# Attention and spectral mixing on one core: the rotary table of the first rows placed ahead of the shift, the first load in four pieces, projections ordered by halves, and three fills placed behind a normalization

## The chip, the core and the metric

The kernel runs on one core of a Trainium2 chip. Five engines work side by side, each through its own queue in order: TensorE (PE) multiplies matrices into PSUM, VectorE (DVE) and ScalarE (ACT) do elementwise work and reductions, GpSimd (POOL) does elementwise work and issues part of the DMAs, and SyncE (SP) only issues DMAs. The metric is the device time of one execution in microseconds (us), as the median of several runs.

## The reference

The input x has shape (2, 2048, 256). Each row is normalized to mean 0 and variance 1. The normalized rows xn go through causal attention with 16 query heads and 4 key and value heads of 16 numbers, with rotary position encoding, and through a spectral mixing layer. Both results are added to x. Cut to what matters:

```python
xn = _layernorm(x)                                   # rows of 256
q, k, v = xn @ wq, xn @ wk, xn @ wv                  # 16, 4 and 4 heads of 16
q, k = _apply_rope(q, cos, sin), _apply_rope(k, cos, sin)
scores = einsum('bshd,bthd->bhst', q, k) / sqrt(16)  # causal, softmax over t
attn_out = einsum('bhst,bthd->bshd', softmax(scores), v) @ wo
y = real(ifft(einsum('bnd,do->bno', fft(xn), w_re + 1j * w_im))) + bias
out = x + attn_out + y
```

## The kernel before

**Blocks and units.** The rows are cut into 8 blocks of 512 (`blocks`, line 78), ordered by position first, so that blocks 0 and 1 are the first 512 rows of the two sequences, blocks 2 and 3 the next 512, and so on. A block is a tile `xt` of 128 partitions with 4 groups (`NI`) of 256 columns. The 16 heads of a block are worked off in 4 units of 4 heads (`units`, line 591). For each unit, TensorE first makes scores with queries on the partitions, from which VectorE takes the row maxima (`maxima`, line 593; tile `sm`). The maxima then enter the second score product as additional rows (`spread`, line 668), whose exponentials ScalarE takes (`scores`, line 693), and `values` (line 767) multiplies them with v.

**From a block of x to queries and keys.** `load_x` (line 166) brings a block in with one DMA from SyncE's queue. `row_stats` (line 233) takes mean and variance on VectorE, one group of 128 rows at a time. `row_power` (line 241) takes the reciprocal root on GpSimd. `row_shift` (line 247) makes the shift on VectorE. `project` (line 379) then holds the pieces of a block: `norm` (four instructions, on VectorE for block 0, on GpSimd for the others), `transpose_x` (TensorE, for each half of the 256 columns, copied by ScalarE into `xnT`), `features` (three products, for K with V and for two halves of Q; each sums over both halves of `xnT`), `other_half` (rotary partners of a feature; with a permutation product in blocks 0 and 1, with DMAs in later ones), `proj_v` (transposes v into the tile `va`), `rotate` and `split` (the rotation and the parting of a float32 into three bfloat16 numbers, seven instructions for each of the three features, on VectorE for block 0, on GpSimd for the others). The parts go by DMA from SyncE's queue into stacked tiles `kst` and `qst` (`stack`, `stack_runs`). `ones` (line 370) fills `va` and four pieces of `kst` of a block with the number one beforehand, on VectorE for block 0 and on GpSimd for the others.

**Tables.** `rotary_table` (line 276) makes the cosines and sines of 512 positions: `expand` on VectorE, eight reductions that read the loaded angles `trig`, and `turn` on TensorE, transposes that ScalarE copies into `cs`. `spectral_matrix` (line 315) makes one matrix out of the two Fourier transforms and the weights, in six pieces on TensorE. `load_late` (line 217) issues the loads for it and for the output product from GpSimd's queue.

**What sets the order.** The order of instructions on each engine is written by a planner when the program is built. It keeps a planned time for each engine (`clock`), planned times at which data or buffers are there (`there`), and rings of buffers (`slots`): the n-th tile of a ring with m buffers waits for the (n-m)-th. `use` adds an instruction's planned cost, `send` that of a DMA, `through_bank` that of a product with the copy of its PSUM bank; the ring `st` of PSUM banks has three. Up to line 1006 instructions are put down as the code reads: a warm-up of 48 transposes on TensorE (line 997), `ones(0)`, statistics, root, late loads, shift, weights. Then `chain` (line 1008) and `table` (line 1033) put the pieces of blocks and tables into streams. A piece has a step of attention from which it may go (`since`), one by which it is due (`by`), its engine, the data that it needs, and the rings from which it takes a buffer. The loop from line 1127 picks the next piece. Off TensorE it takes the piece that could start soonest, and among those within 0.1 us on the same engine the one that is due first. On TensorE it prefers, in turns that depend on how far ScalarE and VectorE are, scores ("B"), row maxima ("A"), due pieces ("F"), values ("V") and pieces that are not due yet ("M"). The chip's engines then follow this order, whatever the real times are.

The pieces of block 0 are due before step 0, those of block 1 by step 1 or a few steps later; the pieces of a later block on TensorE may go in steps `s["pe"] + k // 2`, where k counts them in their list.

Of the kernel before, what the change touches and what calls it, by code (L numbers as in the profile page):

```python
# [23 lines left out]
def tile_attn_plus_spectral_ffn(  # L24
# [29 lines left out]
    nc = tc.nc  # L54
# [11 lines left out]
    NI = SB // P  # L66
# [37 lines left out]
    def slot(tag, more=0):  # L104

        return tag, used[tag] + more - ring[tag]
# [57 lines left out]
    xt = {}  # L164

    def load_x(n):
        send("sp", 512, [slot("xt")], [("xt", "in", n)])
        take_slot("xt")
        xt[n] = work.tile([P, NI, D], F32, tag="xt", bufs=2, name=f"xt{n}")
        nc.sync.dma_start(out=xt[n], in_=block_rows(n))  # L170

    take_slot("qst"), take_slot("qst")
    load_x(0)
# [55 lines left out]


    rstd, shift, mv = {}, {}, {}

    def row_stats(n, i):
        if i == 0:
            mv[n] = work.tile([P, NI, 2], F32, tag="mv", bufs=2, name=f"mv{n}")
        st = work.tile([P, 6], F32, tag="bn", bufs=3, name=f"bn{n}_{i}")
        nc.vector.bn_stats(st, xt[n][:, i, :])
        nc.vector.bn_aggr(mv[n][:, i, :], st)
        use("dve", 0.53, [("xt", "in", n)], [("mv", n)])

    def row_power(n):
        rstd[n] = work.tile([P, NI], F32, tag="rs", bufs=2, name=f"rs{n}")
        nc.gpsimd.tensor_scalar(rstd[n], mv[n][:, :, 1], EPS, None, ALU.add)
        nc.gpsimd.tensor_tensor(rstd[n], rstd[n], neg_half, ALU.pow)
        use("pool", 1.35, [("mv", n)], [("rs", n)])

    def row_shift(n):
        shift[n] = work.tile([P, NI], F32, tag="sh", bufs=2, name=f"sh{n}")
# [27 lines left out]
    def rotary_table(j):  # L276
        ex = []

        def expand():
            at = []  # L280
            for a in range(2):
                ex.append(work.tile([P, NI, P], F32, tag="raw", bufs=3, name=f"trx{j}_{a}"))
                at.append(slot("raw"))
                take_slot("raw")
            for f in range(2):
                for a, e, k in ((0, 0, 0), (0, 1, 0), (1, 0, 2), (1, 1, 1)):
                    cols = f * HP + e * QD
# [5 lines left out]
                    nc.vector.tensor_reduce(  # L293
                        ex[a][:, :, cols : cols + QD].rearrange("p i (d h) -> p i d h", h=NKV),
                        wide.unsqueeze(4), AX.X, ALU.max,
                    )
            use("dve", 1.15, at, [("trx", j)])
            there["trx slots", j] = used["raw"]

        def turn(a):  # L300
            if a == 0:
                cs[j] = work.tile([P, 2, SB], F32, tag="cs", bufs=2, name=f"cs{j}")
            ps = bank(f"ps_tr{j}_{a}")
            for i in range(NI):
                nc.tensor.transpose(ps[:, i * P : (i + 1) * P], ex[a][:, i, :], ident)
# [62 lines left out]
    xnT, va, kst, qst = {}, {}, {}, {}  # L368

    def ones(n):  # L370
        e, eng, us = (nc.vector, "dve", 2.7) if n == 0 else (nc.gpsimd, "pool", 2.5)
        va[n] = const.tile([P, NI, NKV, QD], F32, tag=f"va{n}", name=f"va{n}")
        e.memset(va[n], 1.0)
        kst[n] = const.tile([P, NKV, SB], BF16, tag=f"kst{n}", name=f"kst{n}")
        for h in range(NKV):
            e.memset(kst[n][96:P, h, :], 1.0)
        use(eng, us, (), [("ones", n)])

    def project(n):
# [1 line left out]

        b, j = blocks[n]
        e, eng = (nc.vector, "dve") if n == 0 else (nc.gpsimd, "pool")
        MULT, SUB, CAST, NORM = (0.72, 0.72, 0.46, 0.33) if n == 0 else (1.23, 1.13, 0.63, 0.53)
        raw, sw, swp, part, ra, at = {}, {}, {}, {}, {}, {}
        sends = []
        streams.append(sends)

# [27 lines left out]
            if c == NK - 1:  # L416
                there["xt", n] = clock["pe"]

        def features(c):
            ps = bank(f"ps_q{n}_{c}")  # L420
            for k in range(NK):
                product(
                    ps, wp[:, k, c, :], xnT[n][:, k, :], start=(k == 0), stop=(k == NK - 1)
                )
            raw[c] = work.tile([P, SB], F32, tag="raw", bufs=3, name=f"raw{n}_{c}")
            at[c] = take_slot("raw")
            nc.scalar.copy(raw[c], ps)  # L427
            through_bank(
                1.83, ["wp", *(("xnT", n, k) for k in range(NK))], "act", 0.48, [("raw", "in", n, c)],
                [("raw", at[c] - ring["raw"])],  # L430
            )
            if n >= 2:
                other_half(c)
# [568 lines left out]
        row_stats(0, i)  # L1002
    row_power(0)
    load_late()
    row_shift(0)
    order_weights()

    def chain(n, starts, late=0):

        norms, pe, rot = project(n)  # L1010
        eng = norms[0][0]
        stats = [("dve", [("xt", "in", n)], [], lambda i=i: row_stats(n, i)) for i in range(NI)]
# [273 lines left out]
```

## Time and profile before

| What | us |
|---|---|
| median of 3 runs | 926.1 (925.84 to 926.69) |
| profiled execution, its own time | 926.6 |
| span of that profile, from first to last instruction | 924.9 |
| TensorE busy | 904.8 |
| VectorE busy | 749.3 |
| ScalarE busy | 654.3 |
| GpSimd busy | 370.2 |
| first row maxima product that waits for stacked queries starts at | 32.58 |

The profile describes one execution. In a timeline, each row has the start and the duration in us, the engine (PE is TensorE's products, PEld its weight loads), the line of the kernel, the operation, the tile written and the tiles read, the shape, and how many like instructions the row holds. Brackets give the idle time of the engine before the row and what ended it. In rows of windows, the engines' busy times are followed by the granted clock of TensorE (1.00 is full speed), the busy share of the DMA engines and the rate in GB/s. Matmuls overlap, so that a busy TensorE isn't always at its peak.

### The profile page before, as it was taken

What the parts mean: (1) busy time and instruction counts of PE and PEld (TensorE: products, weight loads), DVE (VectorE), ACT (ScalarE), POOL (GpSimd) and SP (SyncE); (2) the same over time, 40 slices, a digit from 0 to 9 for tenths busy, and PEclk for the clock granted to TensorE, in tenths of its full rate; (3) what the DMA queues carried; (4) which work ended last, traced back from release to release, by engine and by line L of the source; (5) the groups of instructions that cost most, each with busy time, mean ns of one, the idle gap of its engine ahead of it and who ended that gap; (6) DMA issues with size and microseconds to landing.
All of it is one profiled execution on the core that took longest, in us unless ns stands there. A gap on an engine that the chain in (4) does not pass through costs nothing.

```text
span 924.9 us, 39006 instructions
## 1 busy us (share of the span) xinstructions
PE 904.8 (98%) x17324; PEld 499.3 (54%) x17324; DVE 749.3 (81%) x1062; ACT 654.3 (71%) x1381; POOL 370.2 (40%) x556
## 2 busy tenths in 40 slices
PE   7999899999999999999999999999999999999997
PEld 4655565655555555555555555555455554645443
DVE  6878697789779997898995999979789989788601
ACT  3266665588757784888865777858687878588785
POOL 7287666824672414822246520311571021102121
PEclk9999999999999999999999999999999999999999
DMA  5435724351244011440002510010133001100000
GB/s 162 122 88 139 201 84 115 89 141 39 60 117 133 27 38 31 115 128 26 15 27 85 140 38 14 27 60 14 28 107 93 15 3 38 48 15 14 28 1 24
DMA packets 42024, 62.13 MB, mean 67 GB/s; under 512 B 8872, under 2 KB 32152, under 8 KB 41856
## 3 DMA queue, kind: packets, MB, share of 16 engines
q1 hardware_dynamic: 32432, 41.18, 16.7%
q0 software_dynamic: 8128, 17.69, 5.9%
q8 instruction: 135, 2.21, 1.0%
q10 hardware_dynamic: 1296, 0.79, 0.3%
q14 instruction: 33, 0.27, 0.1%
HBM read 32.75 MB, written 18.40 MB: 55 GB/s over the span
## 4 chain that ended last, share of the span: by engine, by line
PE 89%; DVE 4%; ACT 3%; issue 1%; DMA 1%; SPq 1%; POOL 1%; ACTq 0%; DVEq 0%; POOLq 0%
PE av L782 24%; PE st L155 22%; PE sm L155 17%; PE sm L631 7%; PE po L155 6%; PE ps_q L155 4%; DVE mx L636 2%; PE sp L155 2%; PE sm L627 2%; PE st L738 1%; ACT es L745 1%; PE ps_x L411 1%; PE st L734 1%; ACT es L747 1%; SPq L393 1%
## 5 line engine op out<-in xcount | busy, mean ns | idle before, releaser
L636 DVE TENSOR_REDUCE mx<-sm 128x2 f32<-128x1024 f32 (+3 forms) x640 | 649.1, 1058 | 87.7 <-PE sm L631 45.0
L745 ACT ACTIVATE es<-st 128x512 f32<-128x512 f32 (+3 forms) x1194 | 552.4, 543 | 179.7 <-PE st L155 145.5
L155 PE MATMUL st<-qst,kst 115*32 115x512 bf16 (+3 forms) x4264 | 327.1, 354 | 1.1 <-ACT es L745 0.4
L782 PE MATMUL av<-es,va 128*32 128x512 f32 (+3 forms) x2560 | 299.3, 530 | 0.8 <-issue 0.5
L155 PE MATMUL sm<-kst,qst 112*32 112x512 bf16 x3072 | 239.1, 379 | 0.1
L155 PEld LDWEIGHTS <-kst 115*32 115x32 bf16 x4608 | 160.8, 95 | 140.0 <-issue 64.1
L752 POOL TENSOR_SCALAR_AFFINE_SELECT es<-es 128x256 f32<-128x256 f32 x192 | 76.7, 407 | 274.9 <-ACT es L745 233.4
L155 PEld LDWEIGHTS <-qst 112*32 112x32 bf16 x3072 | 96.0, 96 | 93.0 <-issue 65.0
L631 PE MATMUL sm<-kst,qst 112*32 112x32 bf16 (+15 forms) x2048 | 122.0, 280 | 0.8 <-DMA qst<-part 0.8
L627 PE MATMUL sm<-mask,ident_h 128*32 128x64 bf16 (+3 forms) x2048 | 100.0, 201 | 1.2 <-DVE mx L636 0.9
L782 PEld LDWEIGHTS av<-es,va 128*32 128x32 f32 x2560 | 84.7, 109 | 28.3 <-ACT avs L796 2.6
L631 PEld LDWEIGHTS <-qst 112*32 112x32 bf16 x2048 | 66.1, 97 | 34.3 <-issue 20.7
L627 PEld LDWEIGHTS <-ident_h 128*32 128x32 bf16 x2048 | 66.0, 96 | 32.9 <-issue 26.0
L931 DVE TENSOR_TENSOR xr<-po,xr 128x256 f32<-128x256 f32 x36 | 15.3, 424 | 52.3 <-PE po L155 50.4
L817 POOL DMA_DIRECT2D res<-avs x30 | 18.2, 606 | 81.9 <-ACT avs L796 79.3
L155 PE MATMUL ps_q<-xnT,wp 128*32 128x512 f32 x384 | 45.5, 602 | 0.0
L747 ACT ACTIVATE es<-sp 128x1024 f32<-128x1024 f32 (+3 forms) x43 | 36.5, 907 | 7.3 <-PE sp L155 7.2
L427 ACT COPY raw<-ps_q 128x512 f32<-128x512 f32 x24 | 14.1, 586 | 35.1 <-PE ps_q L155 33.9
L518 POOL TENSOR_TENSOR ra<-raw,cs 128x512 f32<-128x512 f32 (+1 forms) x21 | 27.5, 1307 | 24.2 <-ACT raw L427 23.0
L738 PE MATMUL st<-qst,kst 115*32 115x160 bf16 (+15 forms) x512 | 36.4, 281 | 0.4 <-issue 0.4
L155 PE MATMUL po<-wo_sb,attT 128*32 128x256 f32 x512 | 35.0, 380 | 0.7 <-ACT attT L892 0.7
L734 PE MATMUL st<-mask_t,ident_h 128*32 128x128 bf16 (+3 forms) x512 | 30.6, 202 | 4.2 <-issue 3.3
(113 smaller groups left out, 663.0 us busy)
## 6 DMA issues: line engine op xcount, KB each, us to landing
qst<-run SPq DMA_DIRECT2D x62, 128.0 KB
res<-avs POOLq DMA_DIRECT2D x30, 256.0 KB, 2.9
run<-part SPq DMA_DIRECT2D x31, 192.0 KB
qst<-run SPq DMA_DIRECT2D x31, 192.0 KB
xt<-in_L_attn_x_dram SPq DMA_DIRECT2D x8, 512.0 KB
xr<-in_L_attn_x_dram SPq DMA_DIRECT2D x16, 256.0 KB
sw<-raw SPq DMA_DIRECT2D x60, 64.0 KB
attT<-res POOLq DMA_DIRECT2D x15, 256.0 KB, 4.2
```

The lines of the kernel that those rows point to most:

```text
L155: nc.tensor.matmul(to[q : q + QD], lhsT[:, q : q + QD], rhs, start=start, stop=stop)
L518: e.tensor_tensor(ra[c][:r], raw[c][:r], cs[j][:r, 0, :], ALU.mult)
L627: nc.tensor.matmul(to[:, at:wd], ident_h[:, q : q + QD], mask[:, q:], start=True, stop=True, skip_group_check=True,)
L631: nc.tensor.matmul(to[:, : at + QD], rows[:, q : q + QD], keys[:, : at + QD], start=False, stop=True, skip_group_check=True,)
L636: nc.vector.tensor_reduce(t["mx"][:, i, 2 * pr : 2 * pr + 2, k], ps[0][:, :, :wd], AX.X, ALU.max)
L734: nc.tensor.matmul(to[:, lo : at + QD], ident_h[:, q : q + QD], mask_t[:, : q + QD], start=True, stop=True, skip_group_check=True,)
L738: nc.tensor.matmul(to[:, at:], keys[:, q : q + QD], rows[:, at:], start=False, stop=True, skip_group_check=True,)
L745: nc.scalar.activation(es[u, t, pr][:, e, lo:], ps[:, lo:], AF.Exp, scale=SCALE)
L747: nc.scalar.activation(es[u, t, pr][:, :, lo:], wide[pr][:, :, lo:], AF.Exp, scale=SCALE)
L752: nc.gpsimd.affine_select(out=es[u, t, pr][:, :, lo : lo + P], in_=es[u, t, pr][:, :, lo : lo + P], pattern=[[0, 2], [1, P]], compare_op=A ...
L782: nc.tensor.matmul(av[u][QD * h : QD * (h + 1), lo:], va[at_block[b, t // NI]][:, t % NI, h, :], es[u, t, h // 2][:, h % 2, lo:], start=(t ...
L817: nc.gpsimd.dma_start(out=res[n, c][f], in_=avs[u])
```

## The change

The change has these parts.

- `load_x` loads block 0 with four DMAs of 128 rows each, instead of one of 512 rows. Each group's statistics depend on its own DMA. The other blocks keep one DMA.
- The table of the first 512 positions is expanded (`expand`) between `load_late` and `row_shift(0)` in VectorE's order. Before, the planner put it behind `row_shift(0)`.
- `features` becomes a piece for each half of the 256 columns. The first half takes the PSUM bank and needs only the first half of `xnT`, the second half needs the second one and ends with ScalarE's copy. The list of pieces of a block grows by three.
- `ones` of blocks 1, 2 and 3 (and of later ones) needs the last normalized group of block 1, so that the planner puts these fills behind block 1's normalization in GpSimd's order.
- Planned costs change: statistics from 0.53 to 0.6, root from 1.35 to 1.6, `expand` from 1.15 to 1.6, fills on GpSimd from 2.5 to 2.9, normalization of block 1 from 0.53 to 0.8, and two more sends are planned in `load_late`. A half of a feature is planned at 0.9, a whole one was at 1.83.

```diff
     def load_x(n):
-        send("sp", 512, [slot("xt")], [("xt", "in", n)])
+        at = slot("xt")
         take_slot("xt")
         xt[n] = work.tile([P, NI, D], F32, tag="xt", bufs=2, name=f"xt{n}")
-        nc.sync.dma_start(out=xt[n], in_=block_rows(n))
+        step = NI if n else 1
+        for i in range(0, NI, step):
+            send("sp", 128 * step, [at], [("xt", "in", n, k) for k in range(i, i + step)])
+            nc.sync.dma_start(out=xt[n][:, i : i + step, :], in_=block_rows(n)[:, i : i + step, :])
...
         nc.gpsimd.dma_start(out=bias_sb, in_=bias.partition_broadcast(P))
+        send("pool", 256, (), ())
+        send("pool", 128, (), ())
...
-        def features(c):
-            ps = bank(f"ps_q{n}_{c}")
-            for k in range(NK):
-                product(
-                    ps, wp[:, k, c, :], xnT[n][:, k, :], start=(k == 0), stop=(k == NK - 1)
-                )
+        def features(c, k):
+            if k == 0:
+                held[c] = bank(f"ps_q{n}_{c}"), take_slot("st")
+            ps, at_st = held[c]
+            product(ps, wp[:, k, c, :], xnT[n][:, k, :], start=(k == 0), stop=(k == NK - 1))
+            use("pe", 0.9, ["wp", ("xnT", n, k), ("st", at_st - ring["st"])], [("ps", at_st)])
+            if k < NK - 1:
+                return
...
-            pe.append(("pe", ["wp", *table, *xs], ["st", "raw"] + ["sw"] * (n >= 2), lambda c=c: features(c)))
+            pe.append(("pe", ["wp", *table, xs[0]], ["st", "raw"] + ["sw"] * (n >= 2), lambda c=c: features(c, 0)))
+            pe.append(("pe", [xs[1]], [], lambda c=c: features(c, 1)))
...
     row_power(0)
     load_late()
+    table_0 = rotary_table(0)
+    table_0[0]()
     row_shift(0)
     order_weights()
...
-            stream([("pool", [], [], lambda: ones(n))], s["ones"], s["stats"])
+            norm_1 = [("xn", 1, NI - 1)]
+            stream([("pool", norm_1, [], lambda: ones(n))], s["ones"], s["stats"])
...
-        expand, turn = rotary_table(j)
+        expand, turn = rotary_table(j) if j else table_0
         last = [("cs used", at_block[B - 1, j - 2])] if j >= 2 else []
         stream(
-            [("dve", last, ["raw", "raw2"], expand)]
+            [("dve", last, ["raw", "raw2"], expand)] * (j > 0)
             + [("pe", [("trx", j)], ["st"], lambda a=a: turn(a)) for a in range(2)],
```

More of the change, by code (lines that the diff above doesn't have):

```diff
@@ L238, in row_stats @@
         nc.vector.bn_aggr(mv[n][:, i, :], st)
-        use("dve", 0.53, [("xt", "in", n)], [("mv", n)])
+        use("dve", 0.6, [("xt", "in", n, i)], [("mv", n)])
     def row_power(n):
@@ L244, in row_power @@
         nc.gpsimd.tensor_tensor(rstd[n], rstd[n], neg_half, ALU.pow)
-        use("pool", 1.35, [("mv", n)], [("rs", n)])
+        use("pool", 1.6, [("mv", n)], [("rs", n)])
     def row_shift(n):
@@ L296, in expand @@
                     )
-            use("dve", 1.15, at, [("trx", j)])
+            use("dve", 1.6, at, [("trx", j)])
             there["trx slots", j] = used["raw"]
@@ L370, in ones @@
     def ones(n):
-        e, eng, us = (nc.vector, "dve", 2.7) if n == 0 else (nc.gpsimd, "pool", 2.5)
+        e, eng, us = (nc.vector, "dve", 2.7) if n == 0 else (nc.gpsimd, "pool", 2.9)
         va[n] = const.tile([P, NI, NKV, QD], F32, tag=f"va{n}", name=f"va{n}")
@@ L383, in project @@
         e, eng = (nc.vector, "dve") if n == 0 else (nc.gpsimd, "pool")
-        MULT, SUB, CAST, NORM = (0.72, 0.72, 0.46, 0.33) if n == 0 else (1.23, 1.13, 0.63, 0.53)
-        raw, sw, swp, part, ra, at = {}, {}, {}, {}, {}, {}
+        MULT, SUB, CAST, NORM = (0.72, 0.72, 0.46, 0.33) if n == 0 else (1.23, 1.13, 0.63, 0.8 if n == 1 else 0.53)
+        raw, sw, swp, part, ra, at, held = {}, {}, {}, {}, {}, {}, {}
         sends = []
@@ L427, in features @@
             nc.scalar.copy(raw[c], ps)
-            through_bank(
-                1.83, ["wp", *(("xnT", n, k) for k in range(NK))], "act", 0.48, [("raw", "in", n, c)],
-                [("raw", at[c] - ring["raw"])],
+            use(
+                "act", 0.48, [("ps", at_st), ("raw", at[c] - ring["raw"])],
+                [("st", at_st), ("raw", "in", n, c)],
             )
@@ L1011, in chain @@
         eng = norms[0][0]
-        stats = [("dve", [("xt", "in", n)], [], lambda i=i: row_stats(n, i)) for i in range(NI)]
+        stats = [("dve", [("xt", "in", n, i)], [], lambda i=i: row_stats(n, i)) for i in range(NI)]
         stats.append(("pool", [("mv", n)], [], lambda: row_power(n)))
```

## The prediction

> **What bounds the kernel now.** I read the busy shares first, then the head of the timeline (columns: start, duration, engine, line and operation, and in brackets the idle time before it with its releaser), then the same head in one-microsecond windows, then the later windows of 25 us for the rest.
>
> ```profile
> PE 904.8 (98%) x17324; PEld 499.3 (54%) x17324; DVE 749.3 (81%) x1062; ACT 654.3 (71%) x1381; POOL 370.2 (40%) x556
> ...
> 1.41 7.25 PE L997 MATMUL idle<-ident 128*128 128x128 f32 x48 [1.41 <-POOL ident masks.py:199]
> ...
> 5.19 0.43 DVE L237 BATCH_NORM_STATS2 bn<-xt 128x6 f32<-128x256 f32 x1 [0.56 <-DMA xt<-in_L_attn_x_dram]
> ...
> 8.93 0.16 DVE L249 SCALAR_TENSOR_TENSOR sh<-mv,rs 128x4 f32<-128x4 f32 x1 [1.51 <-POOL rs L244]
> 9.01 1.63 DVE L293 TENSOR_REDUCE trx<-trig 128x128 f32<-128x128 f32 x8
> ...
> 10.30 1.09 PE L305 MATMUL ps_tr<-ident,trx 128*128 128x128 f32 x8 [1.64 <-DVE trx L293]
> 10.55 1.89 DVE L399 TENSOR_SCALAR xt<-xt,rs,sh 128x256 f32<-128x256 f32 x4
> ...
> 13.76 2.69 PE L155 MATMUL ps_q<-xnT,wp 128*32 128x512 f32 x16
> ...
> 16.53 0.59 ACT L427 COPY raw<-ps_q 128x512 f32<-128x512 f32 x1 [2.08 <-PE ps_q L155]
> 17.15 0.69 DVE L518 TENSOR_TENSOR ra<-raw,cs 64x512 f32<-64x512 f32 x1 [2.57 <-ACT raw L427]
> ...
> 32.58 0.18 PE L631 MATMUL sm<-kst,qst 112*32 112x32 bf16 x1 [0.81 <-DMA qst<-part]
> ...
> 33.84 0.23 POOL L243 TENSOR_SCALAR rs<-mv 128x4 f32<-128x4 f32 x1 [11.09 <-DVE mv L238]
> 34.15 1.04 POOL L244 TENSOR_TENSOR rs<-rs,neg_half 128x4 f32<-128x4 f32 x1
> 34.23 0.15 DVE L249 SCALAR_TENSOR_TENSOR sh<-mv,rs 128x4 f32<-128x4 f32 x1
> 35.19 4.31 POOL L399 TENSOR_SCALAR xt<-xt,rs,sh 128x256 f32<-128x256 f32 x8
> 37.79 1.01 PE L411 MATMUL ps_x<-ident,xt 128*128 128x128 f32 x4
> ...
> 42.17 1.91 PE L155 MATMUL ps_q<-xnT,wp 128*32 128x512 f32 x16
> ```
>
> ```profile
> 12.00:13.00 1.00, 0.95 (x5) 0.69 (x5) 0.97 (x5) 0.07 (x1) 1.00 (x3) 0.50 0.93 262
> 13.00:14.00 1.00, 1.00 (x8) 0.63 (x10) 0.93 (x5) 0.72 (x2) 0.94 (x3) 0.50 0.95 307
> ```
>
> TensorE is the bound: from 125 us to 875 us nearly every 25 us window has it busy for 24.4 to 25.0. So only time that TensorE loses can be won. It loses it in the head, more than "busy" tells, because a modelled end covers small gaps. I count starts: a feature product takes 1.72 us (the third starts at 22.06, the spectral piece behind it at 23.78), a swap 0.86, a spectral piece 1.73 (23.78 to 25.51), the values' transposes 0.39, one 128x128 transpose 0.071 (seven in each half microsecond late in the warm-up). Between the end of the warm-up (8.66) and 23.78 the work is 8 table and 8 x transposes (1.14), three features (5.16), two swaps (1.72), 0.39: 8.4 of 15.1 us, so **6.7 us are lost**. From 23.78 to 42.17 it is a swap, six spectral pieces (10.4), 16 x transposes (1.14) and the first unit's row maxima (some 2.5): 14.9 of 18.4, so **3.5 more**. Then block 1's projection at last gives TensorE enough to do.
>
> The second loss has one cause. The shift of block 1 (34.23) stands on VectorE behind all of block 0's rotation, since the reciprocal root (18.47 to 19.84) came behind two of GpSimd's fills, and by then rotation pieces, which are due earlier, were always ready. The last windows show half the clock: the two rows end with 0.50 and the DMA columns.
>
> **First load in four.** SyncE's issues stand at 0.80 and 1.31, one per 0.51 us. The pieces go out at 0.80, 1.31, 1.82, 2.33, then the table of angles at 2.85 instead of 1.31 and block 1's load at 3.35 instead of 1.84. VectorE is occupied with fills of 2.11 us from 2.52 until 4.63, so the first statistics start at about 4.68 instead of 5.19: 0.5 us. The fourth piece is needed 1.6 us after that; the whole load was there at 5.1 while issued at 0.80, so three issues later gives 6.6 at worst, and it should be there by 5.5, because it has a quarter of the bytes. The table must land by 6.9. All loads that went out before 2.4 had landed before 8.0 (the last, wv, released ScalarE at 8.09), so it lies between 5.7 and 8.0; order of bytes in SyncE's queue is unchanged, so I take 6. At 8.0 it would take back 1.1 us.
>
> **Table ahead of the shift.** The 1.63 us at 9.01 move into the 1.51 us wait for GpSimd. Statistics end at 6.9, table 6.9 to 8.55, root on GpSimd ready at 8.35, shift 8.55 to 8.7, normalization 8.7 to 10.6 against 12.44. With the load that is **1.85 us**. The table's transposes find their data when the warm-up ends at 8.66 instead of 10.30, and both run before the first normalized row arrives; if they came late, x's transposes would stand behind them.
>
> **TensorE up to the third feature.** x's transposes end near 10.75, the first copy near 11.55, K's feature starts at 11.6 (13.76 before). Weights were ordered by 9.62: covered by 2 us. On the clock: the Trainium skill, "TensorE: Matmul & The Clock Gate", section "What's actually happening", has the gate open after a busy window of about 3.4 us and close after an idle one. Here 0.50 was granted at 12 to 15 us, behind the idle 1.64. In the new order about 45% of the 3.4 us behind the warm-up is work against about 23%. If the rule's window no longer counts as idle, the K feature takes 1.72 and not 2.69, and its third feature ends 3.2 us earlier; if the clock falls as it did, about 2.1. No row shows the threshold, so I take the state of before, **2.1**.
>
> **Fills behind block 1's normalization.** Block 1's statistics end near 12.8 (14.57 before). GpSimd's six load issues still end near 12.85 (13.31 before), then the root, 1.3 us, without two fills of 2.5 ahead of it: 14.2. Following the planner's own costs by hand, K's first rotation product is put down first, then, in the wait for the swap, the shift, then the other six; the margin there is about 0.4 us of planned time. So normalization of block 1 starts near 15 and its x is there by 17.5 instead of 37.4. The three fills (7.5 us) then run until 25. Behind them stand block 1's rotation and block 2's root on GpSimd; block 1's first raw copy, which released that rotation at 44.87, can't come before about 23, so the fills cost it at most 2 us of a gain of some 20. Nothing else is moved past: SyncE's stacks of block 1 come behind block 0's in time (28 and later).
>
> TensorE gets ps_x, three features, three swaps and the values' transposes (9.0 us) from about 20.5 on, next to 10.4 us of spectral pieces: 20 us of cover until 40, when the first unit's maxima have long come. The loss of 3.5 shrinks to about 0.5: **3.0 us**.
>
> A rule speaks against this: the Trainium skill, "SBUF — State Buffer", section "Who interferes with whom", lets a VectorE instruction with two SBUF inputs collide with a GpSimd instruction that reads SBUF. Block 1's normalization (4 x 0.54 on GpSimd) now lies on block 0's K rotation. The row at hand, the addition of K at 19.02 (0.68, under GpSimd's root), shows no stretch against 0.69 alone, but the root reads only four columns. By the rule K's stack, and with it the first maxima, comes up to 2.2 us later (31.6, not 29.4); by the row none. Either way TensorE has projection work until 40, so the sum moves by 0; with that cover gone it would be 2.2.
>
> **Projections by halves.** The 16 products stay the same and the first half already started before the second copy landed (13.76 against 14.45), so on the chip K of block 0 gains nothing. But a half holds one of three rotating PSUM banks. For blocks 2 to 7 the pieces now number nine instead of six, one window per two of them, so that halves of Q0 and of Q1 get different windows: 12 holds. A score head needs a bank and takes 0.54 us of ScalarE (mean 543 ns over 1194 of them). Nothing of before shows such a hold. From both sides: a gain of the same size, since blocks of 1.72 become 0.86, up to a loss of one exponential, 0.54, each (6.5 us); I take 0.04 each, 0.5 in all, as row maxima need no bank.
>
> **The sum.** 2.1 + 3.0 - 0.5 = 4.6 us off the span of 924.9, 920.3; around it lie 1.7 (profiled 926.6). The median of the runs, 926.1, is 0.5 below that execution, so 926.1 - 4.6 = **921.5**.
>
> **Rivals.** (a) The filling is swallowed: only the chain's gain stays, because between 76 and 125 us stalls for ScalarE and VectorE (5.6 us of lost busy time) grow by what block 1 was earlier. For it: those windows are not full. Against it: each of these chains is also fed earlier. 926.1 - 2.0 = 924.1.
> (b) Slower: the held banks. Place: blocks 2 to 7, once all three banks are spoken for; each hold starves ScalarE, then the values. It cancels 5.1 us at 0.43 each and is slower by 0.2% at 0.58, just beyond one exponential. With 0.7 each: 926.1 - 5.1 + 8.4 = 929.4. For it: ScalarE is only 71% busy and waits 145 us for scores already; against it: the planner has other work for TensorE in each of them.
> (c) The shift of block 1 falls behind block 0's rotation once more, since the margin is 0.4. Then the head's 2.1 stays, and 7.5 us of fills come late, in GpSimd's 5.37 us wait at 44.87: 926.1 - 2.1 + 2.1 = about 926.
>
> **How the numbers follow.** Forecast (918.6 to 923.1): 0.57; still faster: 0.02; (a) 923 to 925.5: 0.19; (b) 0.14; (c) 0.08. A difference under 0.2%, 1.85 us, is what measurement can't tell from none. Faster: 0.57 + 0.02 + 0.10 of (a) + 0.02 of (c) = 0.71; same: 0.09 + 0.02 of (b) + 0.04 = 0.15; slower 0.12 + 0.02 = 0.14. The range leaves out the best few and the worse part of (b): 918.0 to 928.0.
>
> **What would show it.** First statistics near 4.7; table reduces directly behind them, no wait before the shift; normalization at 8.7; table transposes at the warm-up's end; K's raw copy 14 to 15.5; block 1's normalization on GpSimd near 15, fills behind it; its ps_x near 20; first row maxima near 30; no GpSimd wait of 11 us. The prediction is wrong if the angles' table lands after 8, if block 1's shift stands behind part of block 0's rotation, or if windows from 125 us on show TensorE below its 24.4 to 25.0.

## The result and the profile after

| | before | after |
|---|---|---|
| median of the runs, us | 925.41 (20 runs) | 921.61 (20 runs, 919.7 to 924.56) |
| ratio, 95% interval | | 0.9965 (0.9953 to 0.9977) |
| profiled execution, its own time, us | 926.6 | 922.81 |
| span of the profile, us | 924.9 | 921.1 |
| TensorE busy in it, us | 904.8 | 900.8 |
| mean granted clock in it | 0.995 | 0.999 |

The kernel became faster by 0.35% (0.23 to 0.47%), about 3.2 us; the forecast was a gain of 4.6. Measured again later beside other kernels, the ratio was 0.9979 (0.9964 to 0.9994). Over all 34 runs of the changed kernel, and 150 of the one before that were timed beside the experiments, the means are 922.03 and 924.85, a gain of 2.8 +- 0.5 us. The experiments below are compared by such means; "+-" is 95% throughout.

The busy row of the page of the changed kernel:

```profile
PE 900.8 (98%) x17324; PEld 497.6 (54%) x17324; DVE 752.9 (82%) x1062; ACT 654.8 (71%) x1381; POOL 372.3 (40%) x556
```

TensorE's busy time fell by 4.0 us with the same 17324 products. Its time outside (span minus busy) went from 20.1 to 20.3 us: no idle time was won in this pair of profiles. What fell is the time of the same work, and the clock has much to do with that. The records of the clock of these two show half speed in stretches of 3.41 us. The profile before has two of them in working time, one over the head (11.95 to 15.36) and one near 107, the profile after has none before its tail. Two such stretches are worth 2 x 3.41 x 0.5 = 3.4 us. Over the runs the difference is smaller: the mean granted clock is 0.9970 before and 0.9983 after, 0.0013 +- 0.0006 apart. Within the runs of one kernel, the time is 0.67 +- 0.09 us shorter for each 0.001 that the clock is higher (359 runs of all the kernels here, each against the mean of its own). An estimate from this slope: 0.9 of the 2.8 us go with the clock, and 2.0 +- 0.4 us are left at equal clock. Whether the new order brings the higher clock is not shown.

The head of the timeline of the changed kernel (start, duration, engine, line, operation, and in brackets the idle time before it with its releaser):

```profile
0.80 1.83 SPq L173 DMA_DIRECT2D xt<-in_L_attn_x_dram  x4
...
4.66 0.43 DVE L242 BATCH_NORM_STATS2 bn<-xt 128x6 f32<-128x256 f32 x1
...
7.03 1.60 DVE L298 TENSOR_REDUCE trx<-trig 128x128 f32<-128x128 f32 x8
...
8.61 1.04 PE L310 MATMUL ps_tr<-ident,trx 128*128 128x128 f32 x8
8.62 0.16 DVE L254 SCALAR_TENSOR_TENSOR sh<-mv,rs 128x4 f32<-128x4 f32 x1
8.81 1.56 DVE L404 TENSOR_SCALAR xt<-xt,rs,sh 128x256 f32<-128x256 f32 x4
...
11.44 1.92 PE L155 MATMUL ps_q<-xnT,wp 128*32 128x512 f32 x16 [0.24 <-ACT xnT L419]
...
13.43 0.58 ACT L434 COPY raw<-ps_q 128x512 f32<-128x512 f32 x1 [1.56 <-PE ps_q L155]
...
14.91 2.82 POOL L404 TENSOR_SCALAR xt<-xt,rs,sh 128x256 f32<-128x256 f32 x4 [0.51 <-DVE sh L254]
...
20.80 0.66 PE L416 MATMUL ps_x<-ident,xt 128*128 128x128 f32 x4
...
29.18 0.18 PE L639 MATMUL sm<-kst,qst 112*32 112x32 bf16 x1
```

One row of its windows (length, then busy time of PE, PEld, DVE, ACT and POOL with counts, granted clock, DMA share, GB/s):

```profile
12.00:13.00 1.00, 1.00 (x16) 0.18 (x8) 0.47 (x2) 0.00 (x0) 0.99 (x2) 1.00 0.88 287
```

Nearly everything up to here came where the forecast put it: statistics at 4.66, the table's reductions directly behind them, no wait before the shift at 8.62, the table's transposes at the end of the warm-up, block 1's normalization on GpSimd at 14.91 with the fills behind it, block 1's `ps_x` at 20.80, the first row maxima product at 29.18 (32.58 before). Only K's raw copy, at 13.43, is earlier than the 14 to 15.5 of the forecast: the clock at 12 to 13 is 1.00, where it was 0.50. The third feature ends at 20.68 (its start, 18.96, and 1.72), 3.1 us earlier than the 23.78 of before.

And there the gain stops. VectorE and GpSimd in the same timeline from 26 us on, and TensorE's products from 34 us:

```profile
26.10 1.28 POOL L525 TENSOR_TENSOR ra<-raw,cs 64x512 f32<-64x512 f32 x1
26.32 1.61 DVE L533 TENSOR_TENSOR raw<-ra,sw 128x512 f32<-128x512 f32 x1
28.37 1.27 POOL L528 TENSOR_TENSOR sw<-sw,cs 64x512 f32<-64x512 f32 x1 [0.99 <-ACT sw L460]
28.42 1.77 DVE L555 TENSOR_TENSOR rb<-raw,part 128x512 f32<-128x512 f32 x1
29.71 1.64 POOL L533 TENSOR_TENSOR raw<-ra,sw 64x512 f32<-64x512 f32 x1
30.22 1.42 DVE L558 CAST part<-rb 128x512 bf16<-128x512 f32 x1
31.68 0.98 DVE L563 TENSOR_TENSOR part<-rb,part 128x512 bf16<-128x512 f32 x1
...
32.58 0.41 DVE L242 BATCH_NORM_STATS2 bn<-xt 128x6 f32<-128x256 f32 x1
...
33.65 0.72 DVE L644 TENSOR_REDUCE mx<-sm 128x2 f32<-128x256 f32 x2
...
34.10 0.22 PE L635 MATMUL sm<-mask,ident_h 128*32 128x128 bf16 x4 [1.81 <-DVE mx L644]
...
34.69 1.07 PE L155 MATMUL ps_sw<-raw,swap 128*32 128x512 f32 x8
```

The same four VectorE instructions in the timeline of the kernel before, where GpSimd stood idle beside them, and what follows on VectorE:

```profile
28.46 0.69 DVE L526 TENSOR_TENSOR raw<-ra,sw 128x512 f32<-128x512 f32 x1
...
29.65 0.69 DVE L548 TENSOR_TENSOR rb<-raw,part 128x512 f32<-128x512 f32 x1
30.38 0.43 DVE L551 CAST part<-rb 128x512 bf16<-128x512 f32 x1
30.84 0.69 DVE L556 TENSOR_TENSOR part<-rb,part 128x512 bf16<-128x512 f32 x1
31.45 0.42 DVE L237 BATCH_NORM_STATS2 bn<-xt 128x6 f32<-128x256 f32 x1
...
33.59 0.72 DVE L636 TENSOR_REDUCE mx<-sm 128x2 f32<-128x256 f32 x2
```

They took 5.78 us in place of 2.50, each while GpSimd ran block 1's rotation. Block 0's rotation ends at 32.66, where it ended at 31.53 before, although its first instruction stands 3.1 us earlier: 4.2 us are lost on VectorE, 3.3 of them here and most of the rest in K's rotation. The first reduction of row maxima stands at 33.65 and stood at 33.59, so nothing of the 3.1 us is left on VectorE, even though only two groups of block 2's statistics stand ahead of it now (1.1 us) and four did before (2.1 us). TensorE then waits for it, as the waits of TensorE from 30 to 60 us (total, times, longest) and the windows of 32 to 34 us say:

```profile
PE sm L635 <- DVE mx L644: 2.1, 2, 1.8
```

```profile
32.00:33.00 1.00, 0.29 (x8) 0.00 (x0) 0.99 (x2) 0.38 (x1) 0.92 (x2) 1.00 0.39 102
33.00:34.00 1.00, 0.00 (x0) 0.00 (x0) 0.94 (x5) 0.00 (x0) 0.66 (x1) 1.00 0.65 173
```

TensorE does nothing from 32.29 to 34.10. Behind the waiting row maxima product stood projection work of block 1 (the swap that ran at 34.69, whose input ScalarE had copied by 31.2), but TensorE took its products in the order written. The windows from 25 to 50 us, before and after:

```profile
25.00:50.00 25.00, 24.02 (x520) 15.00 (x512) 19.84 (x43) 7.44 (x16) 9.41 (x13) 1.00 0.41 106
25.00:50.00 25.00, 22.73 (x533) 14.34 (x522) 22.17 (x39) 7.62 (x17) 20.84 (x24) 1.00 0.41 114
```

TensorE is busy for 1.3 us less in the stretch in which block 1's early projection was to fill it.

### The profile page after: what moved, and what is told of

Same layout as the page of the kernel before. It is cut to its first block, busy times and chain, and to the rows that moved or that the text cites. A ratio compares the mean times of both kernels' runs of the same rounds, so it can differ in the third digit from the quotient of the medians.

```text
span 921.1 us, 39054 instructions
## 1 busy us (share of the span) xinstructions
PE 900.8 (98%) x17324; PEld 497.6 (54%) x17324; DVE 752.9 (82%) x1062; ACT 654.8 (71%) x1381; POOL 372.3 (40%) x556
## 4 chain that ended last, share of the span: by engine, by line
PE 88%; DMA 3%; ACT 3%; DVE 3%; POOL 1%; issue 1%; SPq 0%; ACTq 0%; POOLq 0%; DVEq 0%
PE av L790 24%; PE st L155 23%; PE sm L155 18%; PE sm L639 6%; PE po L155 6%; PE ps_q L155 4%; ACT es L753 2%; PE sp L155 2%; PE sm L635 2%; DMA inv<-sums 1%; PE st L746 1%; PE ps_x L416 1%; ACT es L755 1%; DMA xr<-in_L_attn_x_dram 1%; DMA xt<-in_L_attn_x_dram 0%
## 5 line engine op out<-in xcount | busy, mean ns | idle before, releaser
L155 PEld LDWEIGHTS <-kst 115*32 115x32 bf16 x4608 | 158.8, 95 | 152.2 <-issue 78.0
L639 PE MATMUL sm<-kst,qst 112*32 112x160 bf16 (+15 forms) x2048 | 120.4, 279 | 0.7 <-issue 0.6
L635 PE MATMUL sm<-mask,ident_h 128*32 128x128 bf16 (+3 forms) x2048 | 99.2, 200 | 3.2 <-DVE mx L644 3.0
L155 PE MATMUL ps_q<-xnT,wp 128*32 128x512 f32 x384 | 48.4, 594 | 0.2 <-ACT xnT L419 0.2
L155 PE MATMUL po<-mff,xnT 128*32 128x256 f32 x512 | 34.4, 379 | 0.0
L746 PE MATMUL st<-qst,kst 115*32 115x96 bf16 (+15 forms) x512 | 34.3, 279 | 0.0
```

The costliest lines, as they stand in the source:

```text
L155: nc.tensor.matmul(to[q : q + QD], lhsT[:, q : q + QD], rhs, start=start, stop=stop)
L635: nc.tensor.matmul(to[:, at:wd], ident_h[:, q : q + QD], mask[:, q:], start=True, stop=True, skip_group_check=True,)
L639: nc.tensor.matmul(to[:, : at + QD], rows[:, q : q + QD], keys[:, : at + QD], start=False, stop=True, skip_group_check=True,)
L746: nc.tensor.matmul(to[:, at:], keys[:, q : q + QD], rows[:, at:], start=False, stop=True, skip_group_check=True,)
```

## The experiments

All of them compute the full output. The ratios are those recorded, each against the kernel before timed beside it; they are not quotients of the medians shown. "Slower" is the difference of means to the 34 runs of the changed kernel (negative is faster), and the column behind it is an estimate of the same at equal clock, with the slope above (0.67 us for each 0.001). The groups of kernels were not all timed on the same chip; the kernel before had means of 924.6 to 925.1 us beside them, so differences of half a microsecond between groups say little. No run separates the changed planned costs from the rest of the change.

| Kernel | ratio | 95% interval | median, us | mean granted clock | slower, us | at equal clock, us | first reduction of row maxima at, us |
|---|---|---|---|---|---|---|---|
| after | 0.9965 | 0.9953 to 0.9977 | 921.61 | 0.9985 | | | 33.65 |
| after, again | 0.9979 | 0.9964 to 0.9994 | 921.96 | 0.9981 | | | 32.81 |
| fills free again | 0.9969 | 0.9954 to 0.9983 | 922.44 | 0.9984 | 0.65 +- 0.95 | 0.70 +- 0.69 | 30.34 |
| whole features | 0.9979 | 0.9967 to 0.9992 | 922.96 | 0.9973 | 1.28 +- 0.82 | 0.61 +- 0.69 | 33.54 |
| table behind the shift | 0.9976 | 0.9965 to 0.9987 | 922.52 | 0.9980 | 0.83 +- 0.78 | 0.59 +- 0.46 | 33.88 |
| load in one | 0.9977 | 0.9965 to 0.9988 | 922.38 | 0.9983 | 0.25 +- 0.68 | 0.22 +- 0.53 | 33.26 |
| GpSimd's rotation waits | 0.9949 | 0.9931 to 0.9967 | 921.46 | 0.9980 | with the next | with the next | 29.65 |
| the same, again | 0.9970 | 0.9958 to 0.9982 | 921.33 | 0.9978 | -0.58 +- 0.63 | -0.89 +- 0.53 | 29.93 |
| it waits, whole features | 0.9953 | 0.9939 to 0.9967 | 920.45 | 0.9987 | -1.28 +- 0.81 | -1.05 +- 0.69 | 30.98 |
| load and table alone | 0.9988 | 0.9975 to 1.0002 | 923.97 | 0.9989 | 1.77 +- 0.88 | 2.12 +- 0.83 | 30.95 |
| before, fills held | 1.0060 | 1.0037 to 1.0083 | 930.14 | 0.9968 | 8.26 +- 1.21 | 7.26 +- 1.20 | 36.82 |
| before, 71 transposes | 1.0023 | 1.0011 to 1.0034 | 925.74 | 0.9974 | 4.10 +- 0.79 | 3.48 +- 0.57 | 32.18 |
| before, 61 transposes | 0.9987 | 0.9970 to 1.0003 | 923.77 | 0.9981 | 1.83 +- 1.03 | 1.71 +- 0.86 | 32.06 |
| before | 1 | | 925.41 | 0.9970 | 2.82 +- 0.54 | 1.96 +- 0.37 | 33.59 |

**The fills free again.** In the changed kernel, the fills of blocks 1 to 3 no longer need block 1's normalization.

```diff
-            norm_1 = [("xn", 1, NI - 1)]
-            stream([("pool", norm_1, [], lambda: ones(n))], s["ones"], s["stats"])
+            stream([("pool", [], [], lambda: ones(n))], s["ones"], s["stats"])
```

> The changed kernel with the fills of blocks 1 to 3 free to go ahead of block 1's normalization again; all else as changed. My theory of the prediction (filling TensorE with block 1's projection is worth 3.0 us): about 3 us slower than the changed kernel, 924.6, with block 1's normalization back near 30 us and the row maxima unchanged in start. Rival (what the earlier block 1 gives, GpSimd's collision with VectorE takes back): within 1 us of the changed kernel, and VectorE's last rotation pieces of block 0 last 0.43 to 0.69 us instead of 0.98 to 1.77.

Measured: 0.65 +- 0.95 us slower than the changed kernel. Its timeline, VectorE's last piece of the rotation, the first maxima and GpSimd's normalization of block 1:

```profile
27.59 0.69 DVE L563 TENSOR_TENSOR part<-rb,part 128x512 bf16<-128x512 f32 x1
...
30.34 0.72 DVE L644 TENSOR_REDUCE mx<-sm 128x2 f32<-128x256 f32 x2
...
31.95 0.55 POOL L404 TENSOR_SCALAR xt<-xt,rs,sh 128x256 f32<-128x256 f32 x1
```

Block 1's normalization is back at 31.95, behind block 0's rotation as in the kernel before, so the mechanism that was meant to be worth 3.0 us is undone. VectorE's pieces have their 0.69 again, the first maxima come 3.3 us earlier than in the changed kernel, and the first exponentials on ScalarE start at 45.27 against 48.54. It seems that two things of nearly equal worth change places here, block 1's early projection and the early first unit of block 0; they were not measured apart.

**Whole features.** In the changed kernel, a feature is one piece again, with both products and both needs.

```diff
-            pe.append(("pe", ["wp", *table, xs[0]], ["st", "raw"] + ["sw"] * (n >= 2), lambda c=c: features(c, 0)))
-            pe.append(("pe", [xs[1]], [], lambda c=c: features(c, 1)))
+            pe.append(("pe", ["wp", *table, *xs], ["st", "raw"] + ["sw"] * (n >= 2),
+                       lambda c=c: [features(c, k) for k in range(NK)]))
```

> The changed kernel with each feature as one whole piece again (six pieces in the list of a block). My theory (halves cost 0.5 us): 921.1, 0.5 us faster than the changed kernel, no difference that five rounds show well. Rival b (a held bank costs 0.4 us and more, 12 times): 917 or less. Second rival (halves help by finer pieces): 923 or more.

Measured: 1.28 +- 0.82 us slower than the changed kernel. TensorE's waits from 28 to 40 us:

```profile
PE sm L635 <- DVE mx L644: 2.7, 1, 2.7
```

The halves are a gain here, not the loss that was forecast. But the runs with whole features also had the lower clock, 0.9973 against 0.9983, and at equal clock 0.61 +- 0.69 is left, which is not clear of zero. The profile shows 0.9 us more of waiting at the stall (2.7 against 1.8); in the second profile of the changed kernel the longest wait there is 1.3, so one profile does not fix that difference. The collision is there as before: VectorE's pieces took 1.38, 1.39 and 1.67 us. One of them, though, was not stretched, while GpSimd's instruction beside it was (1.80, where it takes 1.27 alone):

```profile
27.67 0.69 DVE L555 TENSOR_TENSOR rb<-raw,part 128x512 f32<-128x512 f32 x1
27.70 1.80 POOL L528 TENSOR_TENSOR sw<-sw,cs 64x512 f32<-64x512 f32 x1 [0.35 <-DVE part L549]
```

**The table behind the shift.** `expand` of the first table goes back into the planner's stream.

```diff
     table_0 = rotary_table(0)
-    table_0[0]()
     row_shift(0)
...
-            [("dve", last, ["raw", "raw2"], expand)] * (j > 0)
+            [("dve", last, ["raw", "raw2"], expand)]
```

> The changed kernel with the table's expansion behind the shift again; the load in four stays. My theory: normalization of block 0 at 10.1 instead of 8.8 us, TensorE idle again behind the warm-up, 1.35 us slower by the chain alone, 923.0; if the idle brings the clock back to 0.50 at 12 to 15 us, 1.0 more, 924.0. Rival (VectorE paces the start of row maxima and TensorE has cover): under 0.5 us slower, 922.0.

Measured: 0.83 +- 0.78 us slower. Waits of TensorE from 8 to 12 us:

```profile
PE ps_tr L310 <- DVE trx L298: 1.6, 1, 1.6
```

The idle 1.6 us behind the warm-up is back, and block 0's normalization and K's first raw copy stand 1.2 us later in its profile. Yet the clock stayed at 1.00 from 10 to 16 us. So a gap of this length does not by itself bring the half clock.

**GpSimd's rotation waits for VectorE's.** One column of the last part of block 0 is copied by GpSimd ahead of block 1's first rotation, so that the rotation starts when VectorE is through, and the planner is told so.

```diff
+    last_part = {}
...
+                last_part[n, c] = part[c]
...
             if k == 0:
+                if n == 1 and c == NK:
+                    seen = work.tile([P, 1], BF16, tag="seen", bufs=1, name="seen")
+                    nc.gpsimd.tensor_copy(seen, last_part[0, 1][:, 2, 0:1])
...
-                (eng, [("raw", "in", n, c), ("cs", j, 0)], [], lambda c=c: rotate(c, 0)),
+                (eng, [("raw", "in", n, c), ("cs", j, 0)]
+                 + [("part", "in", 0, 1, "l")] * (n == 1 and c == NK), [], lambda c=c: rotate(c, 0)),
```

> The changed kernel, but GpSimd's rotation of block 1 starts only when VectorE has finished block 0's rotation (GpSimd first copies one column of the last part of block 0). If the collision of the two engines stretched VectorE's pieces from 25 to 33 us (1.61, 1.77, 1.42, 0.98 us), they fall back to 0.69, 0.69, 0.43, 0.69, the first reduction of row maxima comes near 30.5 instead of 33.65, TensorE's wait of 1.75 us at 32.3 is gone, and the time is 919 to 920. If something else held them (ScalarE, DMA), they stay long and the time is 921.6 or more.

Its timeline from 26 us on:

```profile
26.31 0.43 DVE L554 CAST part<-raw 128x512 bf16<-128x512 f32 x1
26.77 0.69 DVE L560 TENSOR_TENSOR rb<-raw,part 128x512 f32<-128x512 f32 x1
27.50 0.43 DVE L563 CAST part<-rb 128x512 bf16<-128x512 f32 x1
27.96 0.69 DVE L568 TENSOR_TENSOR part<-rb,part 128x512 bf16<-128x512 f32 x1
...
28.81 0.19 POOL L527 COPY seen<-part 128x1 bf16<-128x1 bf16 x1 [2.94 <-DVE part L568]
28.96 1.28 POOL L529 TENSOR_TENSOR ra<-raw,cs 64x512 f32<-64x512 f32 x1
...
29.65 0.73 DVE L650 TENSOR_REDUCE mx<-sm 128x2 f32<-128x256 f32 x2
```

With the overlap gone, every VectorE piece is back at 0.69 and 0.43, and the first maxima come at 29.65, 4.0 us earlier than in the changed kernel. That shows the cause of the stretch: these instructions slow each other down when they overlap. GpSimd's side gains too: its addition (`raw<-ra,sw`) takes 1.27 in place of 1.64. For the whole kernel it was measured a second time, with the changed kernel beside it:

> GpSimd's rotation of block 1 behind VectorE's rotation of block 0, beside the changed kernel on one chip. If the collision cost TensorE its wait at 32 us: 1 to 2 us faster than the changed kernel. If TensorE finds other waits in its place (row maxima that wait for VectorE later): within 0.5 us of it.

> The changed kernel once more, to stand beside the others of this call: 0.9965 of the kernel before, within 0.9953 to 0.9977. Its pieces of VectorE between 25 and 33 us are stretched as in the first profile.

Over 23 and 34 runs the mean is 921.45 against 922.03, 0.58 +- 0.63 us faster. The 4.0 us on VectorE are worth about 0.6 us at the end, and at most 1.2; at equal clock 0.9 +- 0.5. The same timeline, further on, shows what became of them:

```profile
35.03 1.04 POOL L249 TENSOR_TENSOR rs<-rs,neg_half 128x4 f32<-128x4 f32 x1
...
36.10 0.56 DVE L254 SCALAR_TENSOR_TENSOR sh<-mv,rs 128x4 f32<-128x4 f32 x1 [1.63 <-POOL rs L249]
36.58 3.21 DVE L650 TENSOR_REDUCE mx<-sm 128x2 f32<-128x768 f32 x3
...
37.58 0.22 PE L641 MATMUL sm<-mask,ident_h 128*32 128x128 bf16 x4 [1.46 <-DVE mx L650]
```

GpSimd, which now starts its rotation later, comes to block 2's root at 34.7 to 36.1. Block 2's shift stands in VectorE's queue ahead of the next row maxima and waits for it, 1.63 us; TensorE waits behind that, 1.46. The stall of 1.8 us at 32 us has become one of 1.5 at 36. A kernel that also puts block 2's root ahead of that rotation was not tried.

**It waits, with whole features.** The former kernel, and a feature in one piece as above.

> GpSimd's rotation of block 1 behind VectorE's, and features as whole pieces. If the halves gain by what they put into TensorE's wait for row maxima near 32 us (one idle piece of 2.7 us with whole features, 1.3 to 1.8 with halves), that wait is short here and whole pieces cost nothing: 921.4, as with halves. If halves gain by themselves in blocks 2 to 7: about 922.7. If held banks cost (rival b): 920 or less.

Measured: median 920.45, mean 920.75, 1.28 +- 0.81 us faster than the changed kernel and 0.70 +- 0.79 faster than the same with halves. This is the best version of the study: 0.47% (0.33 to 0.61%) faster than the kernel before. Halving a feature, worth 1.28 without the wait, is worth nothing or less with it; the difference of these two is 1.98 +- 1.14 us. Most of it goes with the clock, though: at equal clock whole features are 0.2 +- 0.8 us faster here and 0.6 +- 0.7 slower without the wait, and 0.8 +- 1.0 between the two is no longer clear.

**Load and table alone.** The changed kernel with free fills and whole features; the planned costs stay as changed.

> Of the change only the load in four, the table ahead of the shift and the planned costs; the fills are free again and features are whole. My theory: 2.1 of 4.6 us, 922.7. If each part gives what its removal took (table 0.8, load 0.3): 923.7. If fills and halves had only undone the collision that they bring (no collision here): 922 or less.

Measured: 923.80 in the mean, 1.05 +- 0.80 us faster than before, 1.77 +- 0.88 slower than the full change. This splits the gain of 2.8 us: 1.05 from load and table, 1.77 from fills and halves together. But these runs had the highest mean clock of all, 0.9989 against 0.9970 before. At equal clock nothing of the first part is seen (0.2 +- 0.8 us slower than before), and fills and halves make 2.1 +- 0.8.

**The fills held in the kernel before.** Only that part of the change, on the kernel before.

```diff
-            stream([("pool", [], [], lambda: ones(n))], s["ones"], s["stats"])
+            norm_1 = [("xn", 1, NI - 1)]
+            stream([("pool", norm_1, [], lambda: ones(n))], s["ones"], s["stats"])
```

> The kernel before with the fills behind block 1's normalization and nothing else. My theory: 3.0 us faster than before, 921.8, if block 1's shift comes ahead of block 0's rotation. If the shift still stands behind the rotation (third rival), or the collision takes the gain back: within 1 us of before, 924 to 925, and row maxima start at 33 us or later.

Measured: 930.14, 0.6% slower than before, against both expectations. Its timeline:

```profile
16.02 2.60 POOL L399 TENSOR_SCALAR xt<-xt,rs,sh 128x256 f32<-128x256 f32 x4 [0.31 <-DVE sh L249]
...
29.38 1.39 DVE L542 CAST part<-raw 128x512 bf16<-128x512 f32 x1
30.80 1.65 DVE L548 TENSOR_TENSOR rb<-raw,part 128x512 f32<-128x512 f32 x1
...
33.23 1.53 DVE L556 TENSOR_TENSOR part<-rb,part 128x512 bf16<-128x512 f32 x1
```

The early normalization came (16.02), and so did the collision. The first reduction of row maxima is at 36.82, 3.2 us later than before, and the first exponentials at 53.33 against 49.68. So of the loss of 5.4 us some 3.7 stand by then. The windows point to where the rest may lie: from 125 to 175 us TensorE is busy for 47.7 us, where it was 49.9 before. Nor is it settled why the same delay of the maxima (3.3 us between the changed kernel and the one with free fills) costs nothing net in the changed kernel.

**More warm-up.** The kernel before with 71 and with 61 transposes in place of 48, to close the idle 1.64 us in front of the table's transposes without moving anything else.

```diff
-    for _ in range(48):
+    for _ in range(71):
```

> The kernel before with 71 instead of 48 transposes in the warm-up, so that TensorE has work until the table comes at 10.3 us; nothing else. If the idle 1.64 us behind the warm-up is what brings the half clock at 12 to 15 us: mean granted clock over the runs up from 0.9971 to some 0.9980 or more, 1.0 us faster than before. If the half clock comes from a window that takes no notice of this gap: no difference, and 0.50 still stands in the windows of some profile.

> The kernel before with a warm-up of 61 transposes, to end near 10.3 us, where the table's transposes start (71 ended at 11.5 and delayed them). If the idle 1.64 us behind the warm-up brings a half clock: mean granted clock 0.998 and about 1 us faster. If not: mean clock 0.9971 and no difference.

With 71 the warm-up ended at 11.5 us, 2.85 later, and pushed the table's transposes from 10.30 to 11.35. That overshot, but it does not explain the 0.23% lost: the clock in that head is 1.00, K's first raw copy comes at 15.59, earlier than before and only 0.12 behind the kernel with 61, which is 2.3 +- 1.1 us faster. What the extra transposes cost stays open. With 61 the gap closed without delay. The windows of that kernel at 12 to 14 us, in the order of columns as above:

```profile
12.00:13.00 1.00, 0.92 (x7) 0.66 (x6) 0.97 (x5) 0.20 (x2) 1.00 (x2) 1.00 0.95 344
13.00:14.00 1.00, 0.76 (x11) 0.19 (x13) 0.93 (x5) 0.92 (x2) 0.94 (x3) 1.00 0.89 262
```

The clock is 1.00 where the kernel before had 0.50, K's first raw copy came at 15.47 in place of 16.53, and the mean was 0.99 +- 0.96 us lower, with the ratio's interval just reaching 1. A gain of that size fits a head at full clock, and at equal clock nothing is left of it (0.3 +- 0.8). Of the 14 profiles of all these kernels, two have the half clock in the head: that of the kernel before, behind the idle 1.64 us, and that of the same kernel with its fills held, behind an idle 1.89. The table behind the shift had an idle 1.58 and no half clock, and the others had no such gap. One profile of each doesn't show that the gap is the cause.

**The load in one piece.** In the changed kernel, `step = NI` for every block.

```diff
-        step = NI if n else 1
+        step = NI
```

> The changed kernel with the first load as one DMA. My theory: statistics start at 5.2 instead of 4.66, and since everything on VectorE stands behind them, 0.5 us slower, 922.1. Rival (a wait further on swallows it): no difference from the changed kernel.

Measured: 0.25 +- 0.68 us slower than the changed kernel. Statistics that start 0.5 us earlier make no difference that shows at the end.

## Why the prediction was right, and where it was not

**Sign and range were right, and so was the mechanism up to 26 us.** 921.6 was measured where 921.5 was forecast. But the reference of the forecast, 926.1, was itself 0.7 above the 925.4 of the later runs, and the gain by ratio is 3.2 us, by all runs 2.8, not 4.6. That the two figures meet is partly luck: the forecast gained 4.6 by order alone at the old clock, while about 2.0 of the measured 2.8 are left at equal clock, 0.9 went with a higher clock that the sum did not count, and the reference of 926.1 stands 1.2 above the mean of the 150 runs. The terms were mis-sized as follows.

**The chain, 2.1.** Up to K's feature (11.44, forecast 11.6) every time was met within about 0.2 us; what differed was the clock. The forecast took "the state of before", the half clock; the profile after has the full clock at 12 to 15 us, and the third feature ended 3.1 us earlier, next to the other value that the text gives, 3.2. So the case at full clock fitted this profile better than the one taken. At the end of the kernel, though, load and table alone were worth 1.05 +- 0.80, half of the term, and nothing that shows at equal clock; taken out of the full change one at a time, the table was worth 0.83 +- 0.78 and the load 0.25 +- 0.68. The step that failed is to count time won in the head in full at the end. The half-clock stretch that the head lost also isn't a fixed cost of before: the runs' mean clock, 0.9970, lies above that profile's 0.995.

**The filling, 3.0.** Its early half was right within half a microsecond of the working (near 15, and about 20.5): normalization at 14.91, `ps_x` at 20.80. Its worth was not: undoing it cost 0.65 +- 0.95. The step that failed is the one on the collision: "Either way TensorE has projection work until 40, so the sum moves by 0". The rule of the Trainium skill, "SBUF — State Buffer", section "Who interferes with whom", spoke against the change and was right in direction. The row set against it, the addition of K under a root that reads four columns, was the wrong neighbour, as the prediction itself half says (it "reads only four columns"). Beyond that:

- the collision was looked for in K's rotation under block 1's normalization. There it was small: two casts and the first subtraction took 0.67, 1.22 and 0.92 us where they took 0.87, 0.45 and 0.68 before, 0.8 us in all against the 2.2 of the rule, and the cast of 1.22 ran beside a fill and not beside the normalization. The first row maxima product still came at 29.18, forecast 29.4. The costly one lies later, in the last rotation of block 0 under block 1's rotation, which the same change brings forward to 26 us. The prediction followed block 1 up to `ps_x` and the fills, and never asked when GpSimd's rotation would then run and beside what;
- the cover didn't hold. Projection work was at hand, but behind a row maxima product in TensorE's order, and TensorE idled for 1.8 us with it in the queue. Cover counts only where it stands ahead of the wait.

That the collision caused the stretch is shown by the kernel in which GpSimd waits: 0.69 and 0.43 again. How much of the missing 2.4 us it cost is less clear, since taking it away gave 0.58 +- 0.63, and 1.28 +- 0.81 together with whole features, and the gain ran into the next wait on VectorE. It is not all of it: without the collision, the filling was worth 1.2 +- 0.9 us (GpSimd's rotation waits, against free fills; 1.6 +- 0.8 at equal clock), still about half of the 3.0. The rest of that term stays unexplained.

**The halves, -0.5.** The sign was wrong in the kernel as changed: undone, they cost 1.28 +- 0.82, or 0.6 +- 0.7 at equal clock. The step that failed is the hold of a PSUM bank, put at 0.04 us for each of 12. The bound on the gain side ("a gain of the same size") was named and passed over. The held banks of rival (b) do not show: the 25 us windows from 125 us to 325 us have TensorE busy for 24.4 to 25.0 us, as before. Once GpSimd waits, whole features are ahead by 0.70 +- 0.79, or 0.2 +- 0.8 at equal clock, which is not clear of zero. Whether the halves help by themselves where the stall stands, or by the clock that those runs had, stays open.

**The rivals.** (a) had the right outcome for the filling (swallowed) by the wrong mechanism: it put the loss between 76 and 125 us, where windows moved little, but it lies at 26 to 34. Its time, 924.1, is excluded, and so is its gain of 2.0 against 2.8 +- 0.5; but it is just what is left at equal clock. (c) did not happen: the shift of block 1 went between block 0's first rotation instructions at 14.66, as worked out by hand.

## What to carry to other kernels

When a change brings work forward on one engine, follow it to its last consumer and list what the other engines do in the new place; work on GpSimd with two large SBUF inputs beside VectorE's can take back what it was to win. Cover on an in-order engine is only what stands ahead of the waiting instruction in its queue. Parts of a change do not add up: here one part alone on the kernel before lost 0.6%, while in the full change it cost nothing. And where differences are near 1 us, the mean clock of the runs is read beside their mean time: here it made up about half of one gain and all of another.

## What was not expected of the hardware

- The size of the collision: a VectorE instruction that overlaps GpSimd's elementwise work took up to 1.1 us longer, with GpSimd's instructions at 1.27 to 1.80. Additions and subtractions with two SBUF inputs went from 0.69 to 1.61 and 1.77 us, and casts from float32 to bfloat16, which have one input, from 0.43 to 1.42. The casts were not in the forecast's wording of the rule; the same section of the Trainium skill names casts in a two-port mode as well. No view here shows the mode in which they ran. Not every overlap stretches VectorE: with whole features one subtraction kept its 0.69, and GpSimd's instruction beside it took 1.80 in place of 1.27.
- The half clock came in stretches of 3.41 us (one of 6.8, at 117 to 124 us in the kernel with the table behind the shift), in some executions and at some places only. An idle 1.64 and 1.89 us behind the warm-up were followed by one in the two profiles with the old head, an idle 1.58 with the table behind the shift by none. One profile is one draw of it, so a head gained in a profile is read against the mean clock of many runs.
